# The recurrence's timetable: layer norm's factors moved to ScalarE, PSUM users moved apart, the first chunk's softplus over two groups

## The chip, the cores and the metric

The kernel runs on one core of one Trainium2 chip. Its time is the device time of that core in microseconds (us). Before the change it takes 3153.62 us, the median of three runs (3153.42 to 3155.03). The core's engines work side by side, each through its own queue in order: TensorE (PE; PEld is its weight load), VectorE (DVE), ScalarE (ACT), GpSimd (POOL), and SyncE (SP), which here only issues DMAs. A wait at the head of a queue holds everything behind it.

## The reference

Two blocks over x of 2 x 2048 x 256 in float32. The first adds causal attention (16 heads) and a mixture of experts to the normalised x. The second is where the change is; with xn the layer norm of x it computes

```
xz = xn @ in_proj.T;  x, z = split(xz)              # 512 channels each
x  = silu(causal_conv4(x) + conv_b)
dt, B, C = split(x @ x_proj.T)                      # 16 + 16 + 16
dt = softplus(dt @ dt_proj.T + dt_b)
h  = exp(dt * A) * h + dt * B * x                   # a step per position, 512 x 16 states
y  = (sum over states of h * C) + x * D
out = x_in + (y * silu(z)) @ out_proj.T + xn @ ternary(weight).T + bias
```

Its input x_in also needs the end of the first block: the two experts' rows of each token are gathered, weighted, added, rotated (`@ rot`) and mixed in by a sigmoid gate.

## The kernel before, in words

The recurrence is the last stage. It works on 8 units: 4 chunks of 512 positions, times 2 batches. A unit is 16 groups (n = 0 to 15, called g0 to g15 here); a group holds four of the 16 states for one block m = n // 4 of 128 channels, as a tile of 128 x 2048. The main loop is written out in issue order, with G running over all 128 groups. In group G it issues:

- `spread_b(G + 1)`: a matmul that spreads B over the partitions into the PSUM tile `bb` (L1708). There is one `bb` and one `uh`, so it waits until VectorE has read the last one.
- `decays(G + 1, q)`, q = 0 to 3: four exponentials on ScalarE (L1697) into one of two `decay` tiles. They can start when the scan of G - 1 has ended and must end before the scan of G + 1.
- on VectorE an add of 128 x 4 (L1809) that puts in the carried state `c0`, then the scan (L1811), and after it `product(G + 1)` (L1721), dt*x times `bb`. 
- on GpSimd the carry copy (L1822) and the product with C (L1823, tile `hh`, three buffers); then on TensorE `summed(G - 1)`, the sum over states into `y` (L1734, L1738), and every fourth group `taken`, a copy of `y` by ScalarE (L1750).

All else of a unit is put between these by a table. The work is written as generators, each `yield` a step: `mix(at)` (24 steps: gathers of the experts' rows L1310, weights L1319, sum L1324, `moT` L1335/L1338, gate L1343 to L1359, rotated rows `pn` L1369/L1376, the other half of the mix L1383/L1386, layer norm L1392 to L1405, transposes `tr` L1413/L1416), `ahead(at)` (input projection `in` L1293/L1432, convolution `cv` L1441/L1450, silu L1456, `xp` L1461/L1468, `dt` L1513/L1518, softplus L1529 to L1555, with two spills of dt and dt*x to DRAM, L1547) and `behind(at)` (`gated` L1561, the previous unit's output `out` L1573 to L1592, `z` L1293/L1614 and its silu L1618). The lists `kinds` say at which group and quarter (n, q) the next step of each flow is issued: flow 0 is `ahead` of the next unit, 1 is `behind`, 2 is `mix` two units ahead, 3 the first ten steps of `mix` three units ahead, 4 the first four of `ahead` two units ahead. `kinds0` is for unit 0, with three more flows: 5 is `mix` of unit 2, 6 the rest of `ahead` of unit 0, 7 the rest of `mix` of unit 1. Quarter 0 lies before the scan, 1 after the second pair of decays, 2 after `summed`, 3 after `product(G + 1)`.

PSUM tiles of all these steps are taken from two buffers (`ps_m`). A tile's reader is not issued at once: `issued` holds it until the next tile is issued or `settle()` is called, so the table also decides where the reader lands in its engine's queue.

The dt and dt*x of a unit come back from DRAM spread over partitions as `dd` (L1662, issued by `spread`, on SP, one block m at a time). For the next unit's first block this is issued in g12. `first` then makes its carried start: `a0` on GpSimd (L1678) in the second-last group before a block, an Exp of it on ScalarE (L1685), and `c0` on GpSimd (L1688) a group later.

Before the loop, `mix(0)`, ten steps of `ahead(0)` and of `mix(1)`, and some more of each run; `ahead(0)` does the softplus of one block of channels and spreads it by matmuls (`over`, L1502/L1505), so that the scan can start before the other three blocks' softplus, which is flow 6 of unit 0.

Of the kernel before, what the change touches and what calls it, by code (L numbers as in the profile page):

```python
# [13 lines left out]
AF = mybir.ActivationFunctionType  # L14
ALU = mybir.AluOpType
# [24 lines left out]
NB = DI // P  # L40
# [1129 lines left out]
def mix_and_state_space(tc, t, col, row, ident, ones, rot, routes, sab, rw, y_d, ab_d, xa_d, out_tiles):  # L1170
# [10 lines left out]
    nc = tc.nc  # L1181
    NC = S // CH
    QT = CH // P
# [3 lines left out]
    with ExitStack() as ctx:  # L1187
# [89 lines left out]
        def settle(n=0):  # L1277
            while len(held) > n:
                take, ps = held.pop(0)
                take(ps)  # L1280
# [21 lines left out]
        def mix(at):  # L1302

            (c, b), m_ = units[at], of[at]
            u = f"{b}_{c}"
            n0 = (b * NC + c) * QT
            ys = one.tile([P, TOP, QT, D], F32, tag="ys", name=f"ys_{u}")
            for i in range(QT):
                for e in range(TOP):
                    nc.gpsimd.indirect_dma_start(  # L1310
                        out=ys[:, e, i, :],
                        out_offset=None,
                        in_=y_d[:, :],
                        in_offset=bass.IndirectOffsetOnAxis(ap=slots[:, e, n0 + i : n0 + i + 1], axis=0),
                    )
                    yield
            for e in range(TOP):
                for i in range(QT):
                    nc.scalar.activation(  # L1319
                        ys[:, e, i, :], ys[:, e, i, :], AF.Copy, scale=wts[:, e, n0 + i : n0 + i + 1]  # L1320
                    )
                yield
            mo = ys[:, 0]
            nc.gpsimd.tensor_tensor(mo, mo, ys[:, 1], ALU.add)  # L1324
            ab = one.tile([P, QT, D], F32, tag="k", name=f"ab_{u}")
            nc.sync.dma_start(ab, ab_d[:, n0 : n0 + QT, :])
            xc = m_["xc"] = xcp.tile([P, QT, D], F32, tag="xc", name=f"xc_{u}")
            nc.sync.dma_start(xc, xa_d[:, n0 : n0 + QT, :])
            yield

            moT = ys[:, 1].rearrange("p (k i) d -> p k (i d)", k=2)
            for k in range(2):
                ps = mm(f"moT_{u}_{k}")
                for i in range(QT):
                    nc.tensor.transpose(  # L1335
                        ps[:, i * P : (i + 1) * P], mo[:, i, k * P : (k + 1) * P], ident
                    )
                issued(ps, lambda ps, k=k: nc.scalar.copy(moT[:, k, :], ps))  # L1338
                yield
            settle()  # L1340

            ps = mm(f"gate_{u}", (P, QT))
            nc.tensor.matmul(ps, lhsT=ident, rhs=sab[:, n0 : n0 + QT], start=True, stop=False)  # L1343
            for i in range(QT):
                for k in range(2):
                    nc.tensor.matmul(
                        ps[:, i : i + 1],
                        lhsT=moT[:, k, i * P : (i + 1) * P],
                        rhs=rw[:, k : k + 1],
                        start=False,  # L1350
                        stop=(i == QT - 1 and k == 1),
                    )
            g = one.tile([P, 2, QT], F32, tag="g", bufs=2, name=f"g_{u}")

            def sigmoid(ps):
                nc.scalar.activation(g[:, 0, :], ps, AF.Exp, scale=-1.0, bias=nmb)
                nc.scalar.activation(g[:, 1, :], g[:, 0, :], AF.Identity, bias=1.0)
                nc.vector.reciprocal(g[:, 0, :], g[:, 1, :])
                nc.scalar.activation(g[:, 1, :], g[:, 0, :], AF.Identity, scale=-1.0, bias=1.0)  # L1359

            issued(ps, sigmoid)
            yield
            settle()
            for h in range(2):
                ps = mm(f"pn_{u}_{h}", (P, 2, D))
                for i in range(2):
                    ts = slice((2 * h + i) * P, (2 * h + i + 1) * P)
                    for k in range(2):
                        nc.tensor.matmul(  # L1369
                            ps[:, i, :], lhsT=moT[:, k, ts], rhs=rot[:, k, :], start=(k == 0), stop=(k == 1)  # L1370
                        )

                def add(ps, h=h):
                    for i in range(2):
                        n = 2 * h + i
                        nc.vector.scalar_tensor_tensor(  # L1376
                            xc[:, n, :], ps[:, i, :], g[:, 0, n : n + 1], xc[:, n, :], ALU.mult, ALU.add
                        )

                issued(ps, add)  # L1380
                yield
            for i in range(QT):
                nc.scalar.activation(ab[:, i, :], ab[:, i, :], AF.Copy, scale=g[:, 1, i : i + 1])  # L1383
            yield
            settle()
            nc.gpsimd.tensor_tensor(xc, xc, ab, ALU.add)  # L1386
            yield

            mv = one.tile([P, QT, 2], F32, tag="mv", bufs=2, name=f"mv3_{u}")
            st = one.tile([P, QT, 6], F32, tag="st", bufs=2, name=f"st3_{u}")  # L1390
            for i in range(QT):
                nc.vector.bn_stats(st[:, i, :], xc[:, i, :])  # L1392
                nc.vector.bn_aggr(mv[:, i, :], st[:, i, :])
            yield
            r = one.tile([P, 2, QT], F32, tag="r", bufs=3, name=f"r3_{u}")
            nc.scalar.activation(r[:, 0, :], mv[:, :, 1], AF.Sqrt, bias=eps)
            nc.scalar.activation(r[:, 1, :], r[:, 0, :], AF.Copy, scale=-1.0)
            nc.vector.reciprocal(r, r)
            nm = one.tile([P, QT], F32, tag="nm", bufs=3, name=f"nm3_{u}")
            nc.gpsimd.tensor_tensor(nm, mv[:, :, 0], r[:, 1, :], ALU.mult)  # L1400
            yield

            n3 = one.tile([P, QT, D], F32, tag="k", name=f"n3_{u}")
            for i in range(QT):
                nc.scalar.activation(  # L1405
                    n3[:, i, :], xc[:, i, :], AF.Identity, scale=r[:, 0, i : i + 1], bias=nm[:, i : i + 1]
                )
            yield
            xnT = m_["xnT"] = two.tile([P, 2, CH], F32, tag="xnT", bufs=3, name=f"xnT_{u}")
            for k in range(2):  # L1410
                ps = mm(f"tr_{u}_{k}")
                for i in range(QT):
                    nc.tensor.transpose(  # L1413
                        ps[:, i * P : (i + 1) * P], n3[:, i, k * P : (k + 1) * P], ident
                    )
                issued(ps, lambda ps, k=k: nc.scalar.copy(xnT[:, k, :], ps))  # L1416
                yield
            settle()
            yield
# [174 lines left out]
        def behind(at):  # L1594
# [30 lines left out]
        places = {}  # L1625
        kinds = (

            [(0, 2), (1, 1), (2, 0), (2, 3), (3, 2), (4, 0), (5, 0), (5, 2), (6, 0), (6, 2)]
            + [(7, 0), (7, 2), (8, 1), (8, 2), (9, 1), (9, 2), (10, 0), (11, 0)],

            [(0, 0), (1, 0), (8, 2), (9, 1), (10, 2), (11, 1), (11, 3), (12, 1), (13, 0)],

            [(0, 2), (3, 0), (3, 3), (4, 2), (6, 3), (7, 2), (8, 1), (9, 0), (9, 3), (11, 2)]
            + [(12, 2), (12, 3), (13, 1), (13, 3)],

            [(n, q) for n in range(8, 12) for q in (0, 2)] + [(12, 3), (13, 3)],

            [(14, 1), (14, 3), (15, 1), (15, 3)],
        )

        kinds0 = (
            [(3, 0), (3, 1), (3, 2), (3, 3), (4, 0), (4, 2), (5, 0), (5, 2), (6, 0), (6, 2), (7, 0)]
            + [(7, 1), (7, 2), (7, 3), (8, 0), (8, 2), (9, 1), (9, 2), (10, 1), (10, 2), (11, 0), (12, 0)],
            kinds[1],
            [(6, 2), (7, 0), (7, 2), (8, 0), (9, 0), (9, 2), (10, 0), (10, 3), (11, 1), (11, 2)]
            + [(12, 2), (12, 3), (13, 1), (13, 3)],
            [(n, q) for n in range(10, 14) for q in (1, 3)] + [(14, 2), (15, 0)],
            kinds[4],
            [(n, q) for n in range(2, 6) for q in (0, 2)] + [(5, 3), (6, 1)],
            [(0, 0)] * 3 + [(0, 1)] * 5 + [(0, 2), (0, 2), (0, 3)],  # L1650
            [(1, 0), (1, 1), (1, 2), (1, 3), (2, 0), (2, 1), (2, 1), (2, 2), (2, 2), (2, 3)],
        )
        for first_chunk, ks in ((True, kinds0), (False, kinds)):
            for kind, where in enumerate(ks):
# [105 lines left out]
        next(aheads[0])  # L1760
        for g in range(4):
            c_rows(0, g)
        for _ in range(4):
            next(mixes[1])
        next(aheads[0])
        for _ in first(0, 0):
# [12 lines left out]
        for G in range(NG):  # L1779
            at, n = divmod(G, NU)  # L1780
# [3 lines left out]
            if n == 0:  # L1784
# [6 lines left out]
                ]  # L1791
                if at == 0:
                    flows += [mixes[2], aheads[0], mixes[1]]
            if n == (1 if G < 4 else 4 * m) and m + 1 < NB:
                spread(at, m + 1)
            if more and n == (12 if at else 13):
                spread(at + 1, 0)
# [135 lines left out]
```

## Time and profile before

One execution was profiled. Its own time is 3152.86 us, 0.76 us below the median of the runs; its span, first to last instruction, is 3151.1 us. The starts of the scans (L1811) give the length of each unit and of each group.

| unit | first scan starts at, us | to the next unit's, us | scan to scan, g0 to g15, us |
|---|---|---|---|
| 0 | 2026.0 | 179.8 | 17.0 15.7 7.1 11.3 11.3 9.3 13.1 7.2 12.5 9.9 9.9 10.0 7.1 9.3 7.6 21.5 |
| 1 | 2205.7 | 137.3 | 7.1 7.2 7.2 7.2 9.4 7.2 10.9 7.2 12.3 11.1 7.5 7.5 7.1 14.2 7.2 7.2 |
| 2 | 2343.0 | 137.2 | 7.1 7.2 7.2 7.2 10.0 7.2 10.9 7.2 11.6 11.1 7.5 7.1 7.1 14.6 7.2 7.2 |
| 3 | 2480.3 | 139.5 | 7.1 7.2 7.2 7.7 11.2 7.2 10.9 7.2 12.0 11.1 7.5 7.1 7.1 14.6 7.2 7.2 |
| 4 | 2619.8 | 139.8 | 7.1 7.2 7.5 7.2 11.7 7.2 10.9 7.2 12.1 11.1 7.5 7.1 7.1 14.6 7.2 7.2 |
| 5 | 2759.6 | 133.3 | 7.1 7.2 7.2 7.2 11.7 7.2 10.9 7.2 12.4 11.1 7.5 7.1 7.1 8.1 7.2 7.2 |
| 6 | 2892.8 | 120.3 | 7.1 7.2 7.2 7.2 7.1 7.2 7.2 7.2 9.1 9.7 7.5 7.2 7.1 8.0 7.2 7.2 |
| 7 | 3013.2 | 138.0 to the end | 7.1 7.2 7.2 7.2 7.1 7.2 7.2 7.2 7.1 8.3 8.5 7.2 7.1 7.2 7.2 28.1 |

How to read it: a group in which VectorE waits for nothing takes 7.1 to 7.2 us (scan 4.42, product 2.30, add 0.17, and the small gaps between). What a group takes beyond that is either more work for VectorE or a wait. Everything before 2026 us, nearly two thirds of the span, is other stages; the change touches them nowhere but in the last 40 us before the first scan.

### The profile page before, as it was taken

The numbers are of one execution on the slowest core, as the hardware profiler recorded it, in microseconds if no ns is written. First come the engines' busy times: TensorE is split into PE (matmuls) and PEld (weight loads), VectorE is DVE, ScalarE is ACT, GpSimd is POOL, SyncE is SP. The second block draws the span as 40 slices with busy tenths as digits, with TensorE's granted clock in tenths as the row PEclk, the third lists the DMA queues.
The fourth block names the chain that finished last, engine by engine and source line by source line (L and its number), as shares of the span: only waits on it lengthen the run. The fifth ranks groups of instructions, "written<-read, shape, count | busy, mean of one in ns | idle before, by whom it ended". The sixth has DMA issues, their size and how long they took to land. (4 is left out here: it accounts for less than half of the span.)

```text
span 3151.1 us, 40126 instructions
## 1 busy us (share of the span) xinstructions
PE 2706.2 (86%) x15159; PEld 1482.8 (47%) x15159; DVE 2045.2 (65%) x2568; ACT 1571.6 (50%) x2485; POOL 1156.8 (37%) x903
## 2 busy tenths in 40 slices
PE   7887888999999999799999996676888878788857
PEld 4543333445444445687888885222323232333213
DVE  6576776887888886332111102367888888889996
ACT  3424555666666666222222222555665656656543
POOL 4213222110110100110111112266787776778775
PEclk9978998999999999999999997777887878789858
DMA  8843222123212300533344542152453534444450
GB/s 287 222 113 78 62 63 64 28 37 61 40 28 28 55 1 15 197 125 123 137 161 174 185 165 68 41 122 75 103 124 79 129 87 105 100 98 100 94 110 17
DMA packets 118791, 307.35 MB, mean 98 GB/s; under 512 B 27424, under 2 KB 69808, under 8 KB 100928
## 3 DMA queue, kind: packets, MB, share of 16 engines
q1 hardware_dynamic: 100448, 209.17, 27.9%
q0 software_dynamic: 16800, 94.38, 8.8%
q8 instruction: 123, 2.02, 0.3%
q10 hardware_dynamic: 1344, 1.16, 0.1%
q14 instruction: 76, 0.62, 0.1%
HBM read 225.74 MB, written 78.91 MB: 97 GB/s over the span
## 5 line engine op out<-in xcount | busy, mean ns | idle before, releaser
L758 ACT ACTIVATE p<-s 128x1024 f32<-128x1024 f32 (+3 forms) x640 | 563.8, 901 | 382.6 <-PE s L750 357.9
L665 DVE TENSOR_REDUCE best<-m 128x2 f32<-128x1024 f32 (+3 forms) x640 | 669.5, 1062 | 110.4 <-PE m L652 99.8
L1811 DVE TENSOR_TENSOR_SCAN hh<-decay,uh 128x2048 f32<-128x2048 f32 x128 | 565.9, 4421 | 41.1 <-ACT decay L1697 28.6
L1823 POOL TENSOR_TENSOR hh<-hh,cc 128x2048 f32<-128x2048 f32 x128 | 579.3, 4526 | 10.9 <-POOL carry L1822 0.7
L705 PE MATMUL pv<-p,v 128*17 128x256 f32 (+1 forms) x4608 | 382.0, 379 | 50.1 <-POOL p L763 47.2
L763 POOL TENSOR_SCALAR_AFFINE_SELECT p<-p 128x256 f32<-128x256 f32 x256 | 103.9, 410 | 785.6 <-ACT p L758 784.4
L1697 ACT ACTIVATE decay<-dd,a_neg 128x511 f32<-128x511 f32 x512 | 331.6, 711 | 80.3 <-DVE hh L1811 79.7
L1133 ACT ACTIVATE hT<-h,b1s 128x256 f32<-128x256 f32 x296 | 138.3, 474 | 390.8 <-PE h L1126 390.8
L1721 DVE TENSOR_TENSOR uh<-dd,bb 128x2048 f32<-128x2048 f32 x128 | 293.7, 2295 | 46.6 <-PE bb L1708 27.0
L1154 DVE COPY yt<-o 128x512 f32<-128x512 f32 x37 | 25.6, 691 | 435.5 <-PE o L1146 435.5
L750 PE MATMUL s<-q,k 64*128 64x512 f32 (+3 forms) x1280 | 288.3, 437 | 22.4 <-DVE best L665 17.3
L1708 PE MATMUL bb<-xp_sb,w_dt 16*128 16x512 f32 x256 | 184.8, 808 | 131.1 <-DVE uh L1721 130.9
L652 PE MATMUL m<-k,q 64*128 64x512 f32 (+3 forms) x1280 | 281.7, 426 | 17.6 <-DVE best L665 8.9
L1126 PE MATMUL h<-xT,w 128*128 128x256 f32 x1184 | 273.9, 385 | 12.0 <-PEq L476 7.3
L1096 POOL DMA_INDIRECT w<-in_w,wrow x74 | 73.1, 988 | 533.5 <-PE h L1126 313.3
L1139 PE MATMUL o<-w,hT 128*128 128x256 f32 x1184 | 265.9, 379 | 0.0
L750 PE MATMUL s<-tops,onesr 64*128 64x512 f32 (+3 forms) x1280 | 248.5, 371 | 0.0
L1126 PEld LDWEIGHTS h<-xT,w 128*128 128x128 f32 x1184 | 224.8, 193 | 46.3 <-DVE xT L1114 8.5
L1738 PE MATMUL y<-hh,sel 128*32 128x512 f32 x1024 | 180.4, 785 | 67.5 <-POOL hh L1823 67.5
L1139 PEld LDWEIGHTS o<-w,hT 128*128 128x128 f32 x1184 | 222.0, 190 | 29.5
L705 PEld LDWEIGHTS pv<-p,v 128*17 128x17 f32 x4608 | 107.6, 97 | 233.0 <-issue 112.2
L750 PEld LDWEIGHTS s<-q,k 64*128 64x128 f32 x1280 | 126.9, 188 | 167.9 <-DVE best L665 56.0
(341 smaller groups left out, 3481.9 us busy)
## 6 DMA issues: line engine op xcount, KB each, us to landing
dd<-dd_d SPq DMA_DIRECT2D x124, 512.0 KB, 8.9
q<-qk_d SPq DMA_DIRECT2D x128, 128.0 KB, 3.7
k<-qk_d SPq DMA_DIRECT2D x128, 128.0 KB, 7.6
x_d<-zero SPq DMA_DIRECT2D x6, 1664.0 KB
xg<-x_d SPq DMA_DIRECT2D x37, 256.0 KB, 2.8
y_d<-yt SPq DMA_DIRECT2D x37, 256.0 KB, 2.1
qk_d<-qp SPq DMA_DIRECT2D x16, 512.0 KB, 3.0
qk_d<-kp SPq DMA_DIRECT2D x16, 512.0 KB, 3.4
```

Source lines behind the costliest of these rows:

```text
L652: nc.tensor.matmul(ps[:, h, 0:n], lhsT=qT[hs, qs], rhs=kT[hs, c * CH : c * CH + n], start=True, stop=True, tile_position=(HP * h, 0),)
L665: nc.vector.tensor_reduce(best[:, i, :, c], ps[:, :, 0:n], AX.X, ALU.max)
L705: nc.tensor.matmul(pv[r0 : r0 + HS + 1, lo - f * HC : HC], lhsT=v[:, b * TPB + kb, 2 * pr + h, :], rhs=pt[:, h, lo:hi], start=(kb == 0), s ...
L750: nc.tensor.matmul(ps[:, h, off:CH], lhsT=(kT[hs, kb * P : (kb + 1) * P], onesr[hs, :])[i], rhs=(qT[hs, j * CH + off : (j + 1) * CH], tp[h ...
L758: nc.scalar.activation(pt[:, :, off:CH], ps[:, :, off:CH], AF.Exp, scale=float(HS) ** -0.5)
L1126: nc.tensor.matmul(ph, lhsT=w1[:, k * DF + f * P : k * DF + (f + 1) * P], rhs=xT[:, k, :], start=(k == 0), stop=(k == 1),)
L1139: nc.tensor.matmul(po[:, h, :], lhsT=hT[:, f, h * P : (h + 1) * P], rhs=w2[:, f * D : (f + 1) * D], start=(f == 0), stop=False,)
L1697: nc.scalar.activation(decay[G % 2][:, q, 1:], of[at]["dd", n // 4][:, 0, q, 1:], AF.Exp, scale=a_neg[:, q, n : n + 1],)
L1708: nc.tensor.matmul(bb[:, 0, :], lhsT=w_dt[DR + DS :, (n % 4) * P : (n % 4 + 1) * P], rhs=of[at]["xp"][DR + DS :, :], start=True, stop=True,)
L1721: nc.vector.tensor_tensor(uh, of[at]["dd", n // 4][:, 1], of[at]["bb", n].to_broadcast(full), ALU.mult)
L1811: nc.vector.tensor_tensor_scan(hh.rearrange("p q c -> p (q c)"), decay[G % 2].rearrange("p q c -> p (q c)"), uh.rearrange("p q c -> p (q c)"),
L1823: nc.gpsimd.tensor_tensor(hh, hh, m_["cc", g].to_broadcast(full), ALU.mult)
```

## The change

- The gate's `reciprocal` on VectorE and the Identity after it leave the held reader `sigmoid` and become plain instructions one step later, ahead of the first `pn`. `mix` has one step more for it.
- Layer norm's mean times minus 1/deviation (`nm`) is made by four ScalarE copies of 128 x 1 in the step that uses it, not by one GpSimd product (L1400) a step earlier.
- In the table of units 1 to 7 the gate's reader, the two `pn`, the mix's last sums, the two `out`, and the layer norm get other places; silu of z goes from (13, 0) to (14, 2); the weights of the gathered rows (L1319) from (12, 3) and (13, 3) to (14, 0) and (15, 0); the convolution's first three steps from (0, 2), (1, 1), (2, 0) to (1, 0), (1, 3), (2, 1).
- In unit 0 the softplus of the other three blocks is spread over groups 0 and 1 (it was all in group 0), the load of `dd` for block 1 goes from g1 to g2, `mix` of unit 1 starts with its gate inside the loop (it was before the loop) and ends in g3 (it was g2), `ahead` of unit 1 starts at (3, 2) and not (3, 0), and the gathers of flow 3 come later.

```diff
@@ mix: gate @@
                 nc.scalar.activation(g[:, 1, :], g[:, 0, :], AF.Identity, bias=1.0)
-                nc.vector.reciprocal(g[:, 0, :], g[:, 1, :])
-                nc.scalar.activation(g[:, 1, :], g[:, 0, :], AF.Identity, scale=-1.0, bias=1.0)
 
             issued(ps, sigmoid)
             yield
             settle()
+            yield
+            nc.vector.reciprocal(g[:, 0, :], g[:, 1, :])
+            nc.scalar.activation(g[:, 1, :], g[:, 0, :], AF.Identity, scale=-1.0, bias=1.0)
             for h in range(2):
@@ mix: layer norm @@
             nm = one.tile([P, QT], F32, tag="nm", bufs=3, name=f"nm3_{u}")
-            nc.gpsimd.tensor_tensor(nm, mv[:, :, 0], r[:, 1, :], ALU.mult)
-            yield
-
+            yield
+
+            for i in range(QT):
+                nc.scalar.activation(nm[:, i : i + 1], mv[:, i, 0:1], AF.Copy, scale=r[:, 1, i : i + 1])
@@ kinds, units 1 to 7: flows 0 to 3 @@
-            [(0, 2), (1, 1), (2, 0), (2, 3), (3, 2), (4, 0), (5, 0), (5, 2), (6, 0), (6, 2)]
+            [(1, 0), (1, 3), (2, 1), (2, 3), (3, 2), (4, 0), (5, 0), (5, 2), (6, 0), (6, 2)]
             + [(7, 0), (7, 2), (8, 1), (8, 2), (9, 1), (9, 2), (10, 0), (11, 0)],
-            [(0, 0), (1, 0), (8, 2), (9, 1), (10, 2), (11, 1), (11, 3), (12, 1), (13, 0)],
-            [(0, 2), (3, 0), (3, 3), (4, 2), (6, 3), (7, 2), (8, 1), (9, 0), (9, 3), (11, 2)]
+            [(0, 0), (1, 0), (8, 3), (9, 3), (10, 3), (11, 1), (11, 3), (12, 1), (14, 2)],
+            [(0, 2), (3, 0), (3, 3), (4, 2), (5, 1), (7, 0), (8, 0), (8, 0), (8, 2), (9, 1), (10, 2)]
             + [(12, 2), (12, 3), (13, 1), (13, 3)],
-            [(n, q) for n in range(8, 12) for q in (0, 2)] + [(12, 3), (13, 3)],
+            [(n, q) for n in range(8, 12) for q in (0, 2)] + [(14, 0), (15, 0)],
             [(14, 1), (14, 3), (15, 1), (15, 3)],
@@ kinds0, unit 0: flows 0, 2, 3, 4, 6, 7 @@
-            [(3, 0), (3, 1), (3, 2), (3, 3), (4, 0), (4, 2), (5, 0), (5, 2), (6, 0), (6, 2), (7, 0)]
-            + [(7, 1), (7, 2), (7, 3), (8, 0), (8, 2), (9, 1), (9, 2), (10, 1), (10, 2), (11, 0), (12, 0)],
+            [(3, 2), (3, 3), (4, 0), (4, 1), (4, 3), (5, 1), (5, 3), (6, 1), (6, 3), (7, 0), (7, 1)]
+            + [(7, 2), (7, 3), (8, 0), (8, 2), (8, 3), (9, 1), (9, 2), (10, 1), (10, 2), (11, 0), (12, 0)],
-            [(6, 2), (7, 0), (7, 2), (8, 0), (9, 0), (9, 2), (10, 0), (10, 3), (11, 1), (11, 2)]
-            + [(12, 2), (12, 3), (13, 1), (13, 3)],
-            [(n, q) for n in range(10, 14) for q in (1, 3)] + [(14, 2), (15, 0)],
-            kinds[4],
+            [(6, 2), (8, 1), (8, 3), (9, 0), (9, 3), (10, 0), (11, 0), (11, 0), (11, 2), (12, 1), (12, 2)]
+            + [(13, 1), (13, 2), (13, 3), (14, 1)],
+            [(11, 3), (12, 0), (12, 2), (13, 0), (13, 2), (14, 0), (14, 1), (14, 3), (15, 1), (15, 2)],
+            [(14, 2), (14, 3), (15, 1), (15, 3)],
-            [(0, 0)] * 3 + [(0, 1)] * 5 + [(0, 2), (0, 2), (0, 3)],
-            [(1, 0), (1, 1), (1, 2), (1, 3), (2, 0), (2, 1), (2, 1), (2, 2), (2, 2), (2, 3)],
+            [(0, 0)] * 3 + [(0, 1), (0, 1), (0, 3), (0, 3), (1, 1), (1, 1), (1, 2), (1, 3)],
+            [(0, 0), (1, 0), (1, 0), (1, 2), (1, 2), (1, 2), (2, 1), (2, 2), (3, 0), (3, 0), (3, 1), (3, 1)],
@@ before the loop, and in it @@
-        for _ in range(4):
+        for _ in range(3):
             next(mixes[1])
-            if n == (1 if G < 4 else 4 * m) and m + 1 < NB:
+            if n == (2 if G < 4 else 4 * m) and m + 1 < NB:
                 spread(at, m + 1)
```

The list of flow 4 for units 1 to 7 stays as it is; unit 0, which shared it, gets one of its own with (14, 2) for (14, 1).

## The prediction

> **What bounds the kernel now.** I read the table of scan starts first, then the busy time unit by unit:
>
> ```profile
> core 0: us, PE busy (x) PEld busy (x) DVE busy (x) ACT busy (x) POOL busy (x), PEclk, DMA share, GB/s
> 2026.00:2205.70 179.70, 122.69 (x332) 44.94 (x328) 127.17 (x79) 104.20 (x158) 117.32 (x68) 0.72 0.36 89
> ...
> 2343.00:2480.30 137.30, 116.25 (x352) 43.57 (x352) 119.09 (x67) 84.29 (x129) 107.67 (x58) 0.81 0.44 104
> ...
> 2892.80:3013.20 120.40, 92.58 (x285) 31.20 (x285) 115.50 (x53) 70.08 (x98) 94.66 (x46) 0.82 0.45 101
> ```
>
> VectorE works 119.1 us in each of units 1 to 5 and no engine more; the unit takes 137 to 140. So the change can win what VectorE waits: 18 to 20 us a unit, some 2 of them the small gaps between its instructions. TensorE (116) and GpSimd (108) are close behind and will bound a unit brought under 120. Next, whom VectorE waits for in units 1 to 4 (releaser, total, times, longest):
>
> ```profile
> DVE hh L1811 <- ACT decay L1697: 21.2, 5, 5.1
> DVE g L1358 <- ACT g L1357: 13.8, 4, 4.6
> DVE xc L1376 <- PE pn L1369: 12.1, 4, 3.0
> DVE uh L1721 <- PE bb L1708: 10.9, 5, 2.8
> DVE xc L1588 <- PE out L1578: 6.2, 4, 1.8
> ```
>
> That is 64.2 us, 16.05 a unit, at five places: the reciprocal (g4), `pn` (g6), `out` (g8), and in g13 first `bb`, then the decays. Why the decays are late is in the same view for ScalarE, and in unit 2 in order of time:
>
> ```profile
> ACT n L1405 <- POOL nm L1400: 25.8, 4, 6.7
> ```
>
> ```profile
> 2453.68 2.07 ACT L1405 ACTIVATE n<-xc,nm,r 128x256 f32<-128x256 f32 x4 [6.07 <-POOL nm L1400]
> ...
> 2460.02 1.28 ACT L1618 ACT_TABLE_LOAD   x1
> 2461.32 1.91 ACT L1618 ACTIVATE zs<-zs 128x2048 f32<-128x2048 f32 x1
> 2463.23 1.28 ACT L1697 ACT_TABLE_LOAD   x1
> 2464.53 1.33 ACT L1697 ACTIVATE decay<-dd,a_neg 128x511 f32<-128x511 f32 x2
> ...
> 2465.95 4.42 DVE L1811 TENSOR_TENSOR_SCAN hh<-decay,uh 128x2048 f32<-128x2048 f32 x1 [5.12 <-ACT decay L1697]
> ...
> 2467.67 0.25 POOL L1678 TENSOR_TENSOR a<-a_neg,dd 128x16 f32<-128x16 f32 x1 [3.31 <-DMA cc<-c_d]
> ```
>
> ScalarE stands 6.07 us for `nm`, a 0.20 us product behind three 4.5 us ones in GpSimd's queue, and then has the sum of two table loads and the silu (4.5 us) ahead of two decays. The last line matters for what comes: `a0` waits for the next unit's `dd`.
>
> **What each part is worth, in units 1 to 4.**
>
> *Gate and `pn`.* The reciprocal is issued two groups after its gate, `pn` is read a group after it is issued: both waits go, 3.45 + 3.0 = 6.5 a unit. Behind the reciprocal at (7, 0) wait only the add and scan of g7; its ScalarE input is made in g5. The second Identity waits for VectorE's product, 2.3 after the scan of g6; two decays (1.3) and Abs (1.9) fill that.
>
> *`out` and z a step later.* `out` is read a group after it is issued: 1.55 gained. Its store on SP stays ahead of the second spill. VectorE's work in g8 and g9 stays (the L1534 and L1539 steps, 2.27 each, layer norm 2.2), so those groups stay at 10 to 12 us.
>
> *`nm` on ScalarE.* Four copies at 0.20 (row L1357, 128 x 4) are 0.8 us and take the place of a 6.07 us wait; the decays' wait in g13 goes, 21.2 / 4 = 5.3. Silu no longer stands there.
>
> *`bb` in g13* is late for another reason: TensorE sits 4.51 us for the product with C of g11 (`y` at 2453.54), since GpSimd is 12 us behind the scan there (gathers, two 4.5 us softplus steps), then does `tr` and `bb`. GpSimd loses only 0.2 us of work and gets the scan of g9 1.6 us earlier. Of 10.9 / 4 = 2.7 I leave 1.5 (bounds 0 and 2.8).
>
> *Silu at (14, 2): a new wait.* There it stands behind the Exp of `a0`, which needs `dd`. Count from the end of g8's scan, E (2411.33 in unit 2). Now the softplus's last product ends at E+36.2 and `dd` lands 19.9 later (2467.45). With `out`'s wait gone GpSimd's chain is 1.6 earlier: `dd` at E+54.5. VectorE alone would start the next unit at E+62.4. ScalarE then does Exp 0.3, a copy 0.56, load 1.28, silu 1.91, load 1.28, four decays 2.6 and, at (15, 0), four row weights 1.7: 9.6, plus 0.7 for `a0`, so E+64.8. VectorE waits 2.4 (bounds: 0 if `dd` lands by E+52, 6 if it lands as late as E+58).
>
> *Convolution at (1, 0).* TensorE now starts it 4.0 us after the unit's first scan (2484.30 in unit 3), works without a gap to 2508.9, and hands over g4's `bb` 0.5 us late. At (1, 0) it comes behind `bb` of g2, which VectorE's product of g1 frees 6.8 after the first scan; with `bb` 1.12 that is 7.9. The 3.9 us go through to g4's product: 4.0 lost. Lower bound 2.1, if the first `cv` took 3.70 as the other three do, not 5.54; upper 5.8, if a second one took 5.54.
>
> The 5.54 is half clock:
>
> ```profile
> 2484.30:2489.90 5.60, 5.60 (x13) 2.30 (x10) 5.36 (x4) 3.04 (x5) 5.52 (x3) 0.67 1.02 221
> 2490.80:2494.60 3.80, 3.80 (x10) 1.81 (x10) 3.53 (x4) 0.39 (x1) 3.72 (x4) 1.00 1.00 207
> 2481.20:2488.00 6.80, 5.57 (x13) 1.84 (x14) 6.56 (x4) 3.04 (x5) 6.72 (x4) 0.50 0.60 140
> ```
>
> It was granted after pauses of 1.20 and 1.35 us; the pause ahead of the moved `cv` will be near 2 us, so I take 5.54 again. [...]
>
> Sum a unit: 16.05 - 1.5 - 2.4 - 4.0 = 8.1; four units 32.6.
>
> **The other units.** Unit 5 waits 4.6 (gate) + 3.0 (`pn`) + 1.9 (`out`) + 1.1 (decays) = 10.6 and has no gathers, so `dd` is in time; it loses 4.0 on `cv`: 6.6. Unit 6 waits 1.0 and loses 4.0: -3.0. Unit 7 and the end (28.1 us after its last scan) stay.
>
> *Before the loop* the gate (TensorE 2007.44 to 2011.45) and its reciprocal (2012.02) stood ahead of `over`; the data of `over` is there at 2008.5. Gain 3.3 (bounds 0 and 3.5). The gate's work goes into g0, where TensorE idles 13 us.
>
> *Unit 0.* The scan of g1 now waits for the whole softplus; spread out, g0 takes 11 and not 17.0, and g1 about 11 and not 15.7. But the last softplus product comes behind two scans' work on GpSimd: 31 us after the first scan and not 23 (2049.1). `dd` of block 1 lands 17.7 later as now (2066.8), at 49 and not 41, and g4 needs it; `a0` holds GpSimd until then, with two gathers (1.0 each) and the products with C of g2 ahead of `c0`: g4's scan at 56 and not 51. Then TensorE sets the pace as now, with `silu` and `xp` further apart from the `bb`s; g9's scan at 103 and not 104.5. The gate's wait in g8 (5.4) is in that. At the end GpSimd has two gathers fewer ahead of the last softplus product, so `dd` for unit 1 lands 4 earlier, but three gathers and silu come behind it: 2.3 back. Net 2 gained, bounds -8 (the later `dd` goes through) and +8.
>
> **Sum.** 32.6 + 6.6 - 3.0 + 3.3 + 2 = 41.5 us off the profiled execution's 3152.86: 3111.4; with the 0.76 by which that execution lies under the median, **3112**. With all bounds against it the units give 16.05 - 2.8 - 6 - 5.8 = 1.5 each and the sum is -2 (6 for the four units, unit 5 4.8, unit 6 -4.8, unit 0 -8): 3156. With all for it 14 each, and 8.5 - 1.1 + 3.5 + 8: 75 off, 3079.
>
> **The rivals.**
>
> *The first `cv` at full clock*, the rest as forecast: 1.9 less lost in units 1 to 6, 11 in all, **3101**. [...] Against: the half clock after pauses of 1.20 and 1.35 us.
>
> *Less is given back*: that, and `dd` in time for silu. Per unit 2.4 + 1.9 more, in units 5 and 6 1.9: 21 more, **3091**. For it: short pauses don't always halve the clock. Against: 19.9 us from product to `dd` in every one of units 1 to 4 (19.7 to 20.8).
>
> *More is given back*, the waits only change place: GpSimd, 108 busy of a unit brought to 130, falls further behind between g9 and g13, `bb` in g13 stays at 2.8, silu's stall is 4 to 5, a second `cv` is at half clock. Per unit 1.3 + 2.1 + 1.8 = 5.2 less, and 3.6 in units 5 and 6: **3136**. For it: GpSimd has no idle time between 2425 and 2464.
>
> *Slower*: silu behind the Exp of `a0`. Each us that `dd` lands after E+54.5 goes straight into units 1 to 4. At E+64.9 the 41.5 are gone; at E+67, 12.5 later, it is 4 x 12.5 = 50: **3162**. Against: `a0` starts at E+56.4 to E+57.4 today, so the load would have to come 7 us later than now with its chain starting earlier.
>
> **How the numbers follow.** The forecast (3104 to 3125) 0.40, `cv` at full clock alone 0.10, less given back 0.17, more 0.20, slower 0.09, and 0.04 for no change, all gains eaten by new waits. A measurement here tells 0.2% (6 us) from no change. Faster 0.87, same 0.04, slower 0.09. The range 3085 to 3141 holds the forecast and most of the two rivals beside it.
>
> **What would show it.** In the changed profile: no wait of L1358, L1376 and L1588 on VectorE; none of L1405 for GpSimd; g13 at 7 to 9 us; a wait of g0's scan for decays at each unit's start, of 2 to 3, with silu after the Exp of `a0`; a wait of g4's product for `bb` of about 4; first scan 3 us earlier; g4 of unit 0 waiting for `dd` till 49 us after it. I am wrong if the wait at a unit's start is over 8, if `cv` holds more than one group, or if unit 0 grows by more than 8.

## The result and the profile after

The changed kernel takes **3135.38 us** (median of 4 runs, 3133.19 to 3138.67), the kernel before 3154.32 beside it (3153.42 to 3155.14): ratio **0.9943**, 95% interval 0.9931 to 0.9955, 18.9 us faster. The forecast was 3112. The sign is right and the time lies in the range, but of the 41.5 us 18.9 came.

The profiled execution of after took 3136.91 us (span 3135.2). Its stages ahead of the change were 4.7 us longer than those in the profile of before (the last `o` of the experts ends at 1928.2, not 1923.5), so I compare from there on: 1227.6 us before, 1207.0 after, 20.6 less. By parts, from the starts of the scans:

| part | before | after | difference | forecast |
|---|---|---|---|---|
| to the first scan | 102.5 | 99.4 | -3.1 | -3.3 |
| unit 0 | 179.8 | 186.6 | **+6.8** | -2 |
| units 1 to 4 | 553.9 | 531.9 | **-21.9** | -32.6 |
| unit 5 | 133.3 | 127.5 | -5.8 | -6.6 |
| unit 6 | 120.3 | 123.5 | +3.2 | +3.0 |
| unit 7 and the end | 138.0 | 138.2 | +0.2 | 0 |

The busy times of units 0, 3 and 6 after (window, its length, then PE, PEld, DVE, ACT, POOL, the granted clock, DMA):

```profile
2027.60:2214.10 186.50, 126.21 (x350) 48.64 (x346) 129.47 (x80) 105.07 (x166) 117.31 (x66) 0.71 0.36 85
2479.80:2612.90 133.10, 116.19 (x350) 44.26 (x350) 118.96 (x66) 84.77 (x133) 106.75 (x57) 0.79 0.45 107
2873.50:2997.00 123.50, 99.52 (x289) 32.97 (x288) 115.39 (x52) 70.85 (x100) 94.49 (x46) 0.77 0.45 99
```

VectorE's work in a unit is the same 119 us, so what a unit of 133 has beyond it is still waiting, but for some 3 us of small gaps between instructions. Whom VectorE waits for after, in units 1 to 4 (the whole list: total, times, longest):

```profile
DVE uh L1723 <- PE bb L1710: 35.3, 16, 3.1
DVE hh L1813 <- ACT decay L1699: 7.5, 4, 2.3
```

Four of the five places of before are empty: no wait for the gate, `pn` or `out`, none for the decays in g13. The fifth, `bb` in g13, has stayed, and the product now waits for `bb` in other groups too. By groups that is g13 11.8, g2 10.3, g3 9.0, g15 3.4, g0 0.8; the decays' 7.5 lie at the units' starts. Per unit: 10.7 us given back where I had 7.9.

### The profile page after: what moved, and what is told of

Read it like the earlier page. It is cut to its first block, busy times and chain, and to the rows that moved or that the text cites. A ratio compares the mean times of both kernels' runs of the same rounds, so it can differ in the third digit from the quotient of the medians.

```text
span 3135.2 us, 40159 instructions
## 1 busy us (share of the span) xinstructions
PE 2712.1 (87%) x15159; PEld 1487.0 (47%) x15159; DVE 2046.9 (65%) x2568; ACT 1574.8 (50%) x2516; POOL 1152.4 (37%) x895
## 5 line engine op out<-in xcount | busy, mean ns | idle before, releaser
L1825 POOL TENSOR_TENSOR hh<-hh,cc 128x2048 f32<-128x2048 f32 x128 | 579.4, 4527 | 10.7 <-POOL carry L1824 0.5
L1133 ACT ACTIVATE hT<-h,b1s 128x256 f32<-128x256 f32 x296 | 138.0, 473 | 392.9 <-PE h L1126 392.9
```

The source lines that it names most:

```text
L1825: nc.gpsimd.tensor_tensor(hh, hh, m_["cc", g].to_broadcast(full), ALU.mult)
```

## The experiments

Each ratio is to the kernel before, run on the same chip. The unit times are from the profiled execution of each; "to the end" is counted from the last `o` of the experts, which leaves out what the earlier stages do; a difference "by the stage" is one of this column, "by the medians" one of the first.

| kernel | median, us | ratio (95%) | to the end | unit 0 | units 1-4 | 5 | 6 |
|---|---|---|---|---|---|---|---|
| before | 3153 to 3155 | 1 | 1227.6 | 179.8 | 553.9 | 133.3 | 120.3 |
| after | 3135.38 | 0.9943 (0.9931-0.9955) | 1207.0 | 186.6 | 531.9 | 127.5 | 123.5 |
| before, gate alone | 3118.23 | 0.9887 (0.9866-0.9908) | 1190.4 | 182.2 | 524.7 | 123.9 | 121.2 |
| before, `nm` alone | 3129.98 | 0.9926 (0.9909-0.9942) | 1202.7 | 177.9 | 536.3 | 127.9 | 120.3 |
| before, gate and `nm` | 3100.46 | 0.9836 (0.9820-0.9853) | 1170.6 | 173.4 | 516.0 | 122.6 | 120.3 |
| after, convolution back | 3117.95 | 0.9888 (0.9871-0.9904) | 1185.9 | 186.1 | 515.6 | 126.2 | 119.4 |
| after, square root earlier | 3133.66 | 0.9932 (0.9916-0.9949) | 1206.9 | 186.2 | 532.2 | 127.5 | 123.6 |
| after, unit 0's softplus back | 3127.19 | 0.9924 (0.9902-0.9946) | 1196.2 | 176.0 | 532.3 | 127.8 | 123.3 |
| after, gathers late | 3134.17 | 0.9930 (0.9914-0.9947) | 1206.4 | 186.6 | 529.8 | 128.9 | 123.8 |
| after, `nm` on GpSimd | 3137.65 | 0.9951 (0.9934-0.9967) | 1210.0 | 189.3 | 532.7 | 127.4 | 123.5 |
| after, silu back in g13 | 3135.20 | 0.9947 (0.9930-0.9963) | 1207.6 | 186.3 | 532.0 | 127.6 | 124.5 |
| after, silu ahead of the Exp | 3116.98 | 0.9878 (0.9862-0.9895) | 1192.8 | 186.1 | 519.1 | 127.2 | 123.4 |
| convolution back, gathers and weights late | 3102.40 | 0.9838 (0.9814-0.9863) | 1177.4 | 186.3 | 505.2 | 128.3 | 119.4 |
| all of the best | 3074.86 | 0.9746 (0.9730-0.9762) | 1152.7 | 179.7 | 493.1 | 123.1 | 119.4 |

### The convolution at its old places

```diff
-            [(1, 0), (1, 3), (2, 1), (2, 3), (3, 2), ...
+            [(0, 2), (1, 1), (2, 0), (2, 3), (3, 2), ...
```

> The changed kernel with the first three convolution steps of units 1 to 7 back at (0, 2), (1, 1), (2, 0). Theory A (the later start of the convolution is what makes the product wait for bb in g2 and g3, 2.6 and 2.3 us in every one of units 1 to 6): those waits fall to 0 to 1 us together, 4 less per unit in six units, time 3111 to 3115. Theory B (TensorE is the bound there whatever the order, as it works without a gap, or the two PSUM buffers make in and cv stand in each other's way): the waits move to another group or to the carried half of in, and the time is within 6 us of 3135.

3117.95: 17.4 less than after by the medians, 21.1 by the stage. The waits in g2 are gone; of those in g3 3.0 of 9.0 us are left in units 1 to 4, and `bb` in g0 costs 3.9 there for 0.8. So Theory A's cause holds, and the time is 3 us above its range; unit 5 got back only 1.3 us. Why the move costs what it does is in TensorE's order. After, in unit 3 (start, duration, and in brackets the idle time before):

```profile
2486.67 2.07 PE L1710 MATMUL bb<-xp_sb,w_dt 16*128 16x512 f32 x2 [2.36 <-DVE uh L1723]
2488.67 5.89 PE L1443 MATMUL cv<-xr,taps 128*128 128x512 f32 x8
...
2496.35 3.70 PE L1443 MATMUL cv<-xr,taps 128*128 128x512 f32 x8
2499.98 1.12 PE L1710 MATMUL bb<-xp_sb,w_dt 16*128 16x512 f32 x2
2501.03 3.70 PE L1443 MATMUL cv<-xr,taps 128*128 128x512 f32 x8
...
2505.66 3.70 PE L1443 MATMUL cv<-xr,taps 128*128 128x512 f32 x8
2509.29 1.12 PE L1710 MATMUL bb<-xp_sb,w_dt 16*128 16x512 f32 x2
```

With the convolution back:

```profile
2473.76 4.27 PE L1443 MATMUL cv<-xr,taps 128*128 128x512 f32 x8
2477.96 1.12 PE L1710 MATMUL bb<-xp_sb,w_dt 16*128 16x512 f32 x2
2479.01 3.70 PE L1443 MATMUL cv<-xr,taps 128*128 128x512 f32 x8
...
2484.50 1.12 PE L1710 MATMUL bb<-xp_sb,w_dt 16*128 16x512 f32 x2
2485.55 3.70 PE L1443 MATMUL cv<-xr,taps 128*128 128x512 f32 x8
...
2490.18 3.70 PE L1443 MATMUL cv<-xr,taps 128*128 128x512 f32 x8
2493.81 1.12 PE L1710 MATMUL bb<-xp_sb,w_dt 16*128 16x512 f32 x2
```

After, two `cv` stand between a `bb` and the next, twice. From `bb` at 2499.98 to `bb` at 2509.29 it is 9.3 us at full clock (granted 1.00 from 2500 to 2512), against VectorE's 7.1: 2.3 lost in g3. The first pair, whose `bb` and first `cv` run for 6.4 us at half clock (granted 0.50 from 2486.6 to 2493.0), takes 13.3 us and loses 2.6 in g2. At the old places one `cv` lies between two `bb`s, twice, and only the last pair comes together. So the loss is not one late hand-over, as I had it, but two groups with two `cv` each.

### The gate's part alone, on the kernel before

```diff
                 nc.scalar.activation(g[:, 1, :], g[:, 0, :], AF.Identity, bias=1.0)
-                nc.vector.reciprocal(g[:, 0, :], g[:, 1, :])
...
             issued(ps, sigmoid)
             yield
             settle()
+            yield
+            nc.vector.reciprocal(g[:, 0, :], g[:, 1, :])
...
-            [(0, 2), (3, 0), (3, 3), (4, 2), (6, 3), (7, 2), (8, 1), (9, 0), ...
+            [(0, 2), (3, 0), (3, 3), (4, 2), (5, 1), (7, 0), (8, 0), (8, 1), (9, 0), ...
```

The Identity behind the reciprocal moves with it, and two lists of unit 0 get one place more for the added step.

> The kernel before with the gate's part alone: the reciprocal two groups behind its gate, `pn` taken a group after it is issued; `out`, z, the layer norm's factors, the convolution, the gathers and unit 0's softplus stay as they were. Theory A, these two waits lie on the path by themselves: 6.5 us less in each of units 1 to 4 and 7.6 less in unit 5, the waits of the reciprocal and of `pn` gone, those of `out`, `bb` in g13 and the decays unchanged: 33 us faster than before, 3121. Rival B, the time comes back within the unit because GpSimd's chain from g8 on is not earlier: the waits for `bb` and for the decays in g13 grow by 3 to 5 a unit, 8 to 18 us faster than before, 3136 to 3146.

34.9 us faster than before, 16 more than the whole change brings. The waits of units 1 to 4:

```profile
DVE hh L1812 <- ACT decay L1698: 20.7, 5, 4.9
DVE uh L1722 <- PE bb L1709: 14.8, 4, 3.8
```

Nothing is left of the gate and `pn`, and `out`'s wait (1.55 a unit) went with them, which I had not expected; `bb` in g13 grew by 1 a unit, so something of Rival B is there, but little.

### `nm` alone, on the kernel before, and with the gate

```diff
-            nc.gpsimd.tensor_tensor(nm, mv[:, :, 0], r[:, 1, :], ALU.mult)
             yield
+            for i in range(QT):
+                nc.scalar.activation(nm[:, i : i + 1], mv[:, i, 0:1], AF.Copy, scale=r[:, 1, i : i + 1])
```

> The kernel before with one part alone: `nm` made by ScalarE in four copies in the step that uses it; every place in the lists as before. Theory A, the 6.07 us that ScalarE stood for `nm` were all that made the decays of g13 late: their wait (5.0 to 5.3 a unit) goes, 20 us faster than before, 3133. Rival B, the silu of z with its two loads, still ahead of these decays, keeps them 2.5 to 3 late, as in the run with the silu back in g13: 8 to 12 us faster, 3142 to 3146. Rival C, `bb` of g13, late by GpSimd's lag, is the next to hold VectorE: under 5 us.

> The kernel before with two parts together: the gate's (which alone gained 35 us) and `nm` on ScalarE (which alone gained 25); the convolution, z, the silu, `out`, the gathers and unit 0's softplus at their old places. Theory A, the two gains are on different waits and add: 60 us faster than before, 3093 to 3098, so that the other moves of the change together cost it some 40 us; `bb` and the decays in g13 (3.7 and 2.7 a unit) are then all that VectorE waits for in units 1 to 4. Rival B, both gains are partly the same microseconds, because GpSimd's lag holds `bb` of g13 back further when the unit gets shorter: 42 to 50 us faster than before, 3105 to 3113, with `bb` of g13 at 5 or more a unit.

`nm` alone gives 24.9 us. The gain is above Theory A's, the waits are Rival B's: 10.8 us for the decays in g13 are left of 20.0 (2.7 a unit, behind the silu of z), and the gate's wait fell from 13.8 to 7.6 and unit 5 by 5.4, so ScalarE was probably earlier for what came next as well. Gate and `nm` together give 52.7 by the medians and 57.0 by the stage; the two alone add to 62.1 by the stage. So they add but for some 5 us by the stage. The median of 3100.46 lies between the two ranges; the waits of units 1 to 4 are those that Theory A named, `bb` in g13 3.7 and the decays in g13 2.7 a unit:

```profile
DVE uh L1723 <- PE bb L1710: 14.8, 4, 3.8
DVE hh L1813 <- ACT decay L1699: 12.0, 5, 2.7
```

**Two parts of the change are worth more than the whole.** Against this kernel, after is 36.4 us longer by the stage: unit 0 13.2, units 1 to 4 15.9, unit 5 4.9, unit 6 3.2, unit 7 2.1, less 2.8 ahead of the first scan.

### Unit 0: two edits

The layer norm's square root for the next mix one step earlier:

```diff
-            [(0, 0), (1, 0), (1, 0), (1, 2), (1, 2), (1, 2), (2, 1), (2, 2), (3, 0), ...
+            [(0, 0), (1, 0), (1, 0), (1, 2), (1, 2), (1, 2), (2, 1), (2, 1), (3, 0), ...
```

> One table entry: in unit 0 the layer norm's square root and reciprocal of mix(1) are issued at (2, 1) and not at (2, 2), so ScalarE has them ahead of the Exp of a0, which waits for block 1's dd. Theory A (VectorE's reciprocal, and behind it the product of g3, stand 21 us because ScalarE's queue is held by that Exp): the 21.3 us wait on L1399 goes, the scan of g3 starts some 20 us earlier, and the wait moves to the product of g4, which itself needs dd (lands 50.6 us after the first scan); g4's scan 6 us earlier than the 62.9 of the changed kernel, and the time 3129. Theory B (the landing of dd alone sets the pace, whoever waits): the wait only changes its name, g4's scan at 62 to 63, the time 3135.

Unit 0's first softplus back in its group, and block 1's spread in group 1:

```diff
-            [(0, 0)] * 3 + [(0, 1), (0, 1), (0, 3), (0, 3), (1, 1), (1, 1), (1, 2), (1, 3)],
+            [(0, 0)] * 3 + [(0, 1)] * 5 + [(0, 2), (0, 2), (0, 3)],
...
-            if n == (2 if G < 4 else 4 * m) and m + 1 < NB:
+            if n == (1 if G < 4 else 4 * m) and m + 1 < NB:
```

> The changed kernel, but unit 0's first softplus keeps its old places (all in the first group) and block 1's spread its old place (group 1). Theory A, the later `dd` of block 1 is what unit 0 pays (it lands 50.6 us after the first scan, some 41 before the change): g4's scan at 51 to 55 and not 62.9, unit 0 at 178 to 182 and not 186.6, units 1 to 6 as in the changed kernel, the time 3127 to 3131. Rival B, unit 0 is set by the layer norm's chain of the next mix and by TensorE, whatever the softplus does: unit 0 stays at 184 to 188 and the time within 2 us of the changed kernel's 3135.

What stands in unit 0 of the changed kernel, in order of time:

```profile
2078.24 0.24 POOL L1680 TENSOR_TENSOR a<-a_neg,dd 128x16 f32<-128x16 f32 x1 [17.72 <-DMA dd<-dd_d]
2078.51 0.22 ACT L1687 ACTIVATE a<-a 128x16 f32<-128x16 f32 x1 [24.83 <-POOL a L1680]
...
2080.37 0.21 ACT L1398 ACTIVATE r<-r 128x4 f32<-128x4 f32 x1
...
2080.61 0.20 DVE L1399 RECIPROCAL r<-r 128x8 f32<-128x8 f32 x1 [21.31 <-ACT r L1398]
```

A chain that I had not seen: `dd` of block 1 lands (50.7 us after the first scan), GpSimd makes `a0`, ScalarE its Exp, and only behind that in ScalarE's queue the square root of the next mix, for which VectorE's reciprocal waits 21.3 us, with the product of g3 behind it in VectorE's queue, though that product needs neither. The square root moved ahead takes this wait away, and the time stays. The waits of VectorE in unit 0 are then:

```profile
DVE uh L1723 <- DMA dd<-dd_d: 20.9, 2, 11.5
DVE uh L1811 <- POOL c L1690: 12.7, 2, 7.0
```

One of the two waits for `dd` is new (11.5, in g3), one of those for `c0` too (5.7); g4's scan starts 59.2 after the first, not 62.8, and these 3.7 are gone by the unit's end in waits for `bb` and for the next unit's `dd`. With the softplus back `dd` is there 8.1 us earlier and unit 0 10.6 shorter, and the wait at the reciprocal is 6.4 with nothing done about it:

```profile
2068.63 0.24 POOL L1680 TENSOR_TENSOR a<-a_neg,dd 128x16 f32<-128x16 f32 x1 [10.65 <-DMA dd<-dd_d]
```

So the softplus spread over two groups, with the later `dd`, is what unit 0 pays; the chain through the layer norm holds at most 3.7 us of it, and these do not reach the unit's end. What stays open is why the 3.7 us go again in the first of the two runs: `bb` in g4 to g6 (2.3, 2.3, 3.1) takes a part, and I did not try what would free it, nor the two edits together.

### The gathers late

```diff
-            [(n, q) for n in range(8, 12) for q in (0, 2)] + [(14, 0), (15, 0)],
+            [(n, q) for n in (8, 9, 12, 13) for q in (0, 2)] + [(14, 0), (15, 0)],
```

> The changed kernel with the last four gathers of flow 3 at (12, 0), (12, 2), (13, 0), (13, 2) and not in g10 and g11 (units 1 to 4 alone have them in that flow). Theory A (bb of g13 is late because GpSimd's queue holds back the product with C of g11, 12.3 us after its scan): with three gathers of 1.1 us fewer ahead of it the lag falls to 9, the wait of the product for bb in g13 from 3.1 to under 0.6, and dd of the next unit lands some 3 earlier, so the wait for decays at the unit's start (1.9) goes too: 4 to 5 less in four units, time 3115 to 3119. Theory B (TensorE's half clock between that product and bb is what counts): the wait stays above 2 and the time within 5 us of 3135.

Theory A has the cause of the wait and Theory B only the time: the wait for `bb` in g13 is gone (11.8 to 0 in units 1 to 4), so GpSimd's lag made it and not TensorE's half clock (granted 0.50 from 2588.3 to 2593.2 after, in unit 3, where `bb` is waited for). But the gain is gone too, since ScalarE now stands for the last gather at the row weights in g14, and the decays behind them cost 9.0 in g14 and 8.5 at the units' starts:

```profile
2600.62 0.51 ACT L1319 ACTIVATE ys<-ys,wts 128x256 f32<-128x256 f32 x1 [7.42 <-DMA ys<-y_d,slots]
```

With the convolution back as well, and these weights at the end of g15:

```diff
-            [(n, q) for n in range(8, 12) for q in (0, 2)] + [(14, 0), (15, 0)],
+            [(n, q) for n in (8, 9, 12, 13) for q in (0, 2)] + [(15, 1), (15, 3)],
```

> The kernel with the convolution at its old places, and in it the last four gathers of mixed rows in groups 12 and 13 and the row weights that read them at the end of group 15 (the run with the gathers alone had ScalarE stand 7.4 us for the last gather at the weights in g14). Theory A, GpSimd's lag was all that made `bb` of g13 late and the weights in g14 were all that took the gain back: `bb` of g13 (3.1 a unit) and the decays at the unit's start (1.7) gone, 12 to 18 us less than the 3118 of that kernel: 3100 to 3106. Rival B, ScalarE's work at the end of the unit (Exp of `a0`, silu, weights, decays) sets the unit's start whatever GpSimd does: 0 to 5 us less, 3113 to 3118.

Theory A, 3102.40. `bb` in g13 and the decays are gone; a wait for `bb` in g0 (2.3 to 3.3 in units 2 to 5) is the largest left. ScalarE stands for `a0` and then does silu, decays and weights ahead of the copy that frees PSUM for the last `in` of the next unit, and TensorE stands for that copy:

```profile
2453.35 0.22 ACT L1687 ACTIVATE a<-a 128x16 f32<-128x16 f32 x1 [6.44 <-POOL a L1680]
...
2463.31 3.78 PE L1293 MATMUL in<-xnT,w_in 128*128 128x512 f32 x4 [4.02 <-ACT xr L1434]
```

### The place of the silu, and the engine of `nm`

The silu of z back at the start of g13, then one step ahead of the Exp of `a0`; both in the changed kernel:

```diff
-            [(0, 0), (1, 0), (8, 3), (9, 3), (10, 3), (11, 1), (11, 3), (12, 1), (14, 2)],
+            [(0, 0), (1, 0), (8, 3), (9, 3), (10, 3), (11, 1), (11, 3), (12, 1), (13, 0)],
```

> The changed kernel with the silu of z back at the start of group 13; z itself stays a step later. Theory A, the place behind the Exp of `a0` costs the wait of 1.9 at each unit's start and the old place is free now that nothing waits for `nm`: that wait goes, none over 0.5 comes in g13, 6 to 8 us faster than the changed kernel, 3127 to 3129. Rival B, the silu and its two table loads, 4.5 us, make the decays of g13 or g14 late by 2 to 3 a unit: no gain or up to 5 us slower, 3135 to 3140.

```diff
-            [(0, 0), (1, 0), (8, 3), (9, 3), (10, 3), (11, 1), (11, 3), (12, 1), (14, 2)],
+            [(0, 0), (1, 0), (8, 3), (9, 3), (10, 3), (11, 1), (11, 3), (12, 1), (14, 1)],
```

> The changed kernel with one place changed: the silu of z at (14, 1), ahead of the Exp of `a0` in ScalarE's queue, instead of (14, 2), behind it. Theory A, the wait for decays in g15 (1.9 a unit in units 1 to 4) is the place behind the Exp and nothing else: it goes, with the 0.85 a unit for `bb` behind it, no new wait, 6 to 11 us less than the changed kernel, 3124 to 3129. Rival B, the decays of g15 wait for `dd` itself, or `cv` a little later takes what is won: the time within 3 us of 3135.

Back in g13 it changes nothing: the wait at the unit's start (7.5) goes, and the decays in g13 cost 10.8 (2.7 a unit), as Rival B has it, with `nm` no longer in the way. One step earlier, at (14, 1), it is 18.4 us less than after by the medians and 14.2 by the stage, more than Theory A had. The wait for the decays is gone in all four units, because the silu and its two loads (1.91 + 2 x 1.28, 4.5 us) now take the time in which ScalarE only waited for `a0`:

```profile
2595.50 1.91 ACT L1620 ACTIVATE zs<-zs 128x2048 f32<-128x2048 f32 x1
...
2598.72 0.22 ACT L1687 ACTIVATE a<-a 128x16 f32<-128x16 f32 x1
```

The Exp runs at 2598.72 without a wait; in the changed kernel it had one of 3.28 and the silu came behind it. So one place in a list, not the later step as such, was the price. What it gives beyond the 7.5 is in `bb`: g2, g13 and g15 have 5 us less.

```diff
+            nc.gpsimd.tensor_tensor(nm, mv[:, :, 0], r[:, 1, :], ALU.mult)
             yield
-            for i in range(QT):
-                nc.scalar.activation(nm[:, i : i + 1], mv[:, i, 0:1], AF.Copy, scale=r[:, 1, i : i + 1])
```

> The changed kernel with nm made by GpSimd's one product again, in the step of the square root, which the new table has at (10, 2). Theory A (what helped is that the step moved from (11, 2) to (10, 2), ahead of the second 4.5 us softplus product and the product with C of g11 in GpSimd's queue; the engine matters little): no wait of the normalised rows for nm over 1 us, time within 3 us of 3135. Theory B (the engine is what helped: GpSimd is behind from g8 on): the rows wait several us for nm, TensorE's tr and bb of g13 come later, 3 to 5 more in each of units 1 to 4, time 3147 to 3155.

3137.65, units 1 to 4 532.7 against 531.9; the 3.0 us more by the stage are nearly all in unit 0 (189.3 for 186.6). With the square root's step a group earlier, the engine matters little in units 1 to 4: GpSimd has time to get to `nm`.

### All of the best

Gate, `pn`, `out` and `nm` as changed; the convolution, and unit 0's softplus, at their old places; gathers and weights late; the silu at (14, 1).

> Gate, `pn`, `out` and `nm` as in the changed kernel; the convolution at its old places, gathers and row weights late as in the run at 3102, unit 0's softplus at its old places, and the silu of z one step earlier, at (14, 1), ahead of the Exp of `a0` and not behind it. In the run at 3102 ScalarE stood 6.4 us ahead of that Exp, the last `in` of the next unit waited for ScalarE's copy, TensorE idled 4.0 us, and the first product of units 2 to 5 waited 2.2 to 3.2 for `bb`. Theory A, silu with its two loads (4.5 us) fits into the 6.4: these waits go, 8 to 11 us less, and unit 0 is 10 shorter: 3080 to 3086. Rival B, `dd`'s landing and the decays behind it set the unit's start whatever silu does: only unit 0's 10 us: 3091 to 3094.

**3074.86 us** (3073.37 to 3078.38), 0.9746 (0.9730 to 0.9762): 80 us faster than before and 60 faster than the change, more than Theory A had. Unit 3 takes 122.7 for 118.9 of VectorE's work, and this is all that VectorE waits for in units 1 to 4 over 0.6 us:

```profile
2449.70:2572.40 122.70, 105.54 (x351) 40.49 (x350) 118.91 (x66) 84.83 (x134) 106.48 (x57) 0.87 0.50 116
```

```profile
DVE uh L1723 <- PE bb L1710: 1.0, 1, 1.0
```

Unit 0, with 179.7 against 173.4 in the kernel with gate and `nm` alone, is not as good as it could be.

## Why the prediction was wrong in size

**What held.** Four of the five waits named are gone, and `bb` in g13, of which the forecast left a part, has stayed. The three terms outside units 0 to 5 are met: 3.1 us for 3.3 ahead of the first scan, +3.2 for +3.0 in unit 6, +0.2 for 0 in unit 7. The new wait at a unit's start is there, 1.9 for 2.4, but its size is in part luck. Counted from E, the end of g8's scan, `a0`, which needs `dd`, starts at E+54.8 to E+55.4, where I had `dd` at E+54.5. In unit 3 ScalarE's decays end at E+66.2, not E+64.8, and VectorE, held by `bb` in g13 and g15, is there at E+64.4, not E+62.4: both came later, and the difference stayed. The four waits that went are not where the error lies; the gate's part alone gave more than its 6.5, since the 1.55 that I gave to moving `out` came with it. A small part of the sum was misread: of the 64.2 us, 1.2 of the decays' lie at the start of unit 1 and 0.6 of `bb`'s in g3, not in g13.

**The step that failed most: unit 0.** "Net 2 gained" was 6.8 lost, 8.8 of the 20.9 us that are missing and more than any other term. I had "g4's scan at 56 and not 51": it came at 62.8. `dd` landed 1.7 later than I had it (50.7 for 49), and from there to the scan I gave 7, where the kernel took 12.1: the chain of `a0`, Exp and square root to VectorE's reciprocal, with g3's product behind it. From g4's scan to the end of the unit I had 121.8 and it took 123.8. The premise beneath it, that the later `dd` is mostly absorbed because "TensorE sets the pace as now", is what the run with the softplus back refutes: `dd` 8.1 earlier made the unit 10.6 shorter. That the lower bound was "-8 (the later `dd` goes through)" shows that the case was seen and judged unlikely.

**Units 1 to 4: what is given back.** 10.7 a unit, not 7.9, and so 5.5 net for 8.1; 10.7 us in the four units.
- "Of 10.9 / 4 = 2.7 I leave 1.5" for `bb` in g13: it was 3.0. I had GpSimd 1.6 earlier; its chain gained 0.7. That this lag is the cause is shown by the gathers moved late, which take the whole wait away.
- "4.0 lost" for the convolution: 4.8, in two groups. I had counted one delay handed on; the cause is two `cv` between two `bb`s, 9.3 us against 7.1, and in the first of the two groups the half clock (granted 0.50) as well, which holds `bb` too (2.07 for the 1.12 that I had). Undone, it gives back 21.1 us over the stage, near my 24.
- A wait for `bb` in g15, 0.85 a unit, was in no term.

**The rivals.** "More is given back", 3136, met the time, and of its mechanisms one: `bb` in g13 stayed near 2.8. Silu's wait did not reach 4, no second `cv` was at half clock (all six took 3.70, granted 1.00), and the largest loss, in unit 0, was not in it, so that its time came out right was luck. "Slower", behind the Exp of `a0`, was the right place but never near the E+64.9 at which the gains would have been gone.

**The first `cv`'s clock.** I took 5.54 from unit 3 of before and said that it followed short pauses. The value was right for after (5.30 to 5.93 in all six units, granted 0.62 to 0.69), the reading of before was not: there the first `cv` took 3.70 in five of six units (granted 1.00), after pauses just ahead of up to 1.35. So half clock is not what was there already but part of what the move costs, 1.6 to 2.2 us in five of the six units. It holds for the first part of that `cv` only: all of it at 0.50 would be, by my estimate from the 3.70 at 1.00, twice that, 7.4. The granted clock after, up to 1.6 us before that `cv` ends in unit 3, is 0.50:

```profile
2486.60:2493.00 6.40, 6.33 (x7) 2.34 (x8) 6.16 (x4) 1.30 (x3) 6.32 (x6) 0.50 0.92 197
```

The pause just ahead of that `bb` and `cv` was 1.34 to 2.36 us in units 1 to 5 and 3.46 in unit 6, where the `cv` took the least, 5.30.

## What to carry to other kernels

When a change bundles moves, price each against the queue it lands in: the two edits that took waits away were worth 53 us by themselves, and places in lists moved along with them cost some 35 of these. The silu put behind an Exp that waited for a transfer inherited that wait (1.9 us a unit in units 1 to 4), and one place earlier the same work was free; ask of each moved step what stands just ahead of it on its engine, and how much of one engine's work lies between two hand-overs to the engine that bounds. A wait that disappears when the step under it is moved, while the time stays (21.3 us at the reciprocal in unit 0, 3133.66 us for 3135.38), may be only the name of another delay; undo the suspected cause, not the wait.

## What the runs showed of the hardware

That the first `cv` takes such different times after one and the same pause was not expected. After a pause of 1.34 to 1.35 us, with one group of matmuls between, it took 3.70 (before, unit 6, granted 1.00), 5.54 (before, unit 3, 0.66) and 5.60 (after, unit 1, 0.66): 1.90 us between the ends for one and the same pause, so the pause just ahead does not decide alone. Nor did a longer pause just ahead go with a longer `cv`: after, 1.39 in unit 2 was followed by 5.93 and 3.46 in unit 6 by 5.30. With gathers and weights late it took 5.66 in unit 3, with a pause of 4.02 ahead of the last `in` before it. No run here shows what else decides.
